# Graph layers with residual norms, fp32: adjacency rows loaded ahead of x and summed later, transposes queued on their own, another order for the first two aggregations and for the last softmax

## The chip, the cores and the metric

The kernel runs on one core of one Trainium2 chip. The metric is the device time of one execution in microseconds (us), the median of several. The groups of runs were made on different chips, and their medians of the kernel before differ by up to 0.3% (1958.9 us in one, 1961.8 to 1964.8 us in the others), so kernels of different groups are compared by their ratio to the kernel before in the same rounds.

Engines are named as in the profile: PE (TensorE, matmuls), PEld (its weight loads), DVE (VectorE), ACT (ScalarE), POOL (GpSimd), SP (it issues the DMA transfers). A line of a timeline has start and duration in us, engine, line of kernel.py, operation, tiles written<-read, shapes, and xN where N instructions are merged. L90 is the helper that issues the work of ACT, DVE and POOL, L173 is the matmul (L177 where an experiment's kernel has four lines more above it).

Tiles: y and v are sums of products of layer 0 and layer 1; own is the output of layer 0 while it is built up, z the half of layer 0's aggregation that is kept apart from own; fifth is the copy of one of the seven products, to be added elsewhere; xT is x transposed, x1T the transposed output of layer 0; xT_s, xT_i, x1T_s, x1T_i, sa and tv are the sums and differences that the seven products need of xT, x1T, adj and y.

## The reference

64 graphs of 256 nodes with 512 features. Two layers, each with a residual and a layer norm:

```python
# layer 0
deg = sum(adj, -1);  agg = (adj @ x) / max(deg, 1e-6)
x = layernorm(x + relu(concat([x, agg]) @ W.T))
# layer 1
q, k = split(x @ Wqk);  v = x @ Wv
agg = adj @ (k * mask)
w = inv_scale * mask * sum(q * agg, -1)
x = layernorm(x + softmax(w, over the nodes)[:, None] * v)
```

## The kernel before

It takes the graphs in 32 pairs. Layer 0 of pair j is interleaved with layer 1 of pair j-1. Products of 2x2 blocks are done with seven multiplications in place of eight (two levels deep for some), so between the matmuls there are many small sums: on ACT (copies from a PSUM bank to SBUF or to another bank), on DVE (additions), on POOL (sums of inputs). A unit of the lists below ("i", "k", "s") is one or two calls of `mm`, and each call shows as two matmul instructions in the trace.

The matmuls stand in a fixed order. The work of the norms, softmaxes and row sums is put between them by a small scheduler that runs while the program is built: chains of steps with a rank; after each unit, `tick` issues the first step whose engine, by a simple cost model, will be free in time. On the chip every engine then takes its instructions in that order.

```python
    act = InOrder(tc, nc.scalar, clock,
                  lambda name, n: 0.07 + n / 1200 if name == "copy" else 0.2 + n / 1000)
    ...
    def tick():
        while not quiet[0]:
            for c in list(chains):
                if c[2][0] <= clock[0] and c[3][0][0].free <= clock[0] + room[c[3][0][0]]:
                    step(c)
                    break
            else:
                return
```

The row sums of adj (the degrees) are made on ACT from a tile "turn", the transposes of the finished layer-0 output go into a tile of the same name and from there by 16 transfers into x1T:

```python
    def degrees(j):
        ...
        def degree(k, t):
            act.activation(r[:, k, t], r[:, k, t], AF.Copy, accum_out=deg[:, k, t:t + 1])
        ...
        queue(2, "degrees", ...four of them..., (vec, invert))

    def norm0(j):
        ...
            turns = [(vec, lambda k=k, t=t: turn(k, t)) for t in range(NT)] if j < NP - 1 else []
            queue(1, "norm", *work, *norm_of(own[:, k], total), *turns)
```

The loop over the pairs (j > 1):

```python
            run("i k", i=i, k=k)
            send_scores(j - 2)
            run("i l k", i=i, k=k, l=open1)
            flush("norm")                       # what is left of the norm, transposes last
            fetch_scores(j - 2)
            places[0](range(16))                # turn -> x1T
            run("i k i k", i=i, k=k)
        ...
            load_x(j)
            load_rows(j + 1)
        ...
        run("m p p m p p m", m=m, p=p)          # p: first products with xT_s ("S2")
        ...
        queue(1, "sums", *sums_Y)               # sums of x1T
        T = sums_T(ys[j])                       # four differences tv (T1 to T4) from y
        degrees(j + 1)
        ...
        run("s s j s a b j c d j k e j", s=s, j=jj, k=k, **g)   # a to g: the aggregation
```

In the aggregation (`gather`), a and b end with additions to own on DVE; those of a read the bank that d writes again. d also needs T2, e needs T3, g needs T4.

## Time and profile before

| | kernel before |
|---|---|
| time | 1958.9 us median (1958.2 to 1963.1, 4 runs) |
| busy: PE, DVE, ACT, POOL | 96%, 79%, 67%, 46% |
| time lost between matmuls, all | 102.3 us |
| of it 0 to 45 / 45 to 63 / 63 to 105 us | 4.8 / 10.6 / 9.5 us |
| of it in the 28 pairs up to the last | 65.5 us |
| after the last matmul's end | 15.6 us |

"Lost" is the time between the starts of neighbouring matmuls less what it is undisturbed, as the prediction tells. The "28 pairs" are the same 28 x 216 matmuls in every kernel of this document, so the sums can be compared directly. (In the kernel before they run from 246 to 1903 us, a pair later than those of the prediction; hence 65.5 us here and 66.5 there.)

The prediction shows the shares, waits and timelines of this kernel.

### The profile page before, as it was taken

To read this page: it belongs to the slowest core of one execution; us is meant where nothing else is said; L and a number is where in the kernel's file an instruction comes from. 1 tells how busy PE (TensorE), PEld (TensorE's weight loads), DVE (VectorE), ACT (ScalarE), POOL (GpSimd) and SP (SyncE) were. 2 spreads that over 40 slices of the span, in tenths; PEclk is the share of its full clock that TensorE was granted. 3 is DMA by queue.
4 is the path that set the end of the run, shared out by engine and by line. 5 is a ranking of instruction groups with operands and counts; after the bars stand their busy time and mean duration, and the time that the engine had idled before them with its cause. 6 is when DMAs were issued, how large, how long until landed. Compare 5 with 4: busy or idle time off the path is not lost.

```text
span 1958.7 us, 24833 instructions
## 1 busy us (share of the span) xinstructions
PE 1882.4 (96%) x6980; PEld 1310.1 (67%) x6980; DVE 1556.1 (79%) x3185; ACT 1304.8 (67%) x3267; POOL 896.1 (46%) x1187
## 2 busy tenths in 40 slices
PE   9899999999999999999999999999999999999995
PEld 4567666667666676666676666666666666666674
DVE  7678877878787788878788878788878787878786
ACT  3467766676766676666776676777676766666775
POOL 4354534544435554435544445444345444355531
PEclk9899999999999999999999999999999999999998
DMA  6132343423343323333323333323434323434211
GB/s 216 37 75 94 88 112 81 113 74 96 91 114 82 101 81 100 92 92 103 83 94 99 98 93 102 79 94 87 113 82 113 78 93 90 113 81 113 72 53 49
DMA packets 389160, 182.30 MB, mean 93 GB/s; under 512 B 272160, under 2 KB 353696, under 8 KB 389024
## 3 DMA queue, kind: packets, MB, share of 16 engines
q1 hardware_dynamic: 389024, 180.72, 34.4%
q8 instruction: 57, 0.93, 0.2%
q14 instruction: 79, 0.65, 0.1%
HBM read 114.10 MB, written 34.06 MB: 76 GB/s over the span
## 4 chain that ended last, share of the span: by engine, by line
PE 64%; SPq 11%; DMA 9%; ACT 7%; DVE 7%; issue 2%; POOL 0%; ACTq 0%; DVEq 0%
PE bank L173 64%; SPq L178 11%; DMA turn<-adj 6%; DMA x1T<-turn 3%; ACT junk L90 2%; ACT turn L90 2%; ACT bank L90 2%; DVE own L90 1%; DVE v L90 1%; DVE tv L90 1%; DVE y L90 1%; ACT own L90 1%; DVE turn L90 1%; ACT rstd L90 1%; DMA xT<-x_t 1%
## 5 line engine op out<-in xcount | busy, mean ns | idle before, releaser
L90 ACT COPY bank<-bank 128x256 f32<-128x256 f32 (+1 forms) x768 | 336.1, 438 | 218.1 <-PE bank L173 211.2
L90 DVE TENSOR_TENSOR y<-bank,y 128x512 f32<-128x512 f32 x256 | 170.5, 686 | 144.2 <-ACT y L90 138.6
L90 ACT ACTIVATE junk<-own,less 128x512 bf16<-128x512 f32 x252 | 181.7, 721 | 62.4 <-DVE less L90 59.4
L173 PE MATMUL bank<-tv,sa 128*128 128x256 f32 x768 | 199.4, 388 | 6.9 <-DVE own L90 3.1
L90 ACT ACTIVATE own<-own,shift,rstd 128x512 f32<-128x512 f32 x256 | 198.5, 812 | 3.4 <-DVE shift L90 3.4
L90 POOL TENSOR_TENSOR x1T_s<-x1T,x1T_s 128x512 f32<-128x512 f32 x32 | 48.5, 1517 | 316.5 <-PE bank L173 316.5
L173 PEld LDWEIGHTS bank<-tv,sa 128*128 128x128 f32 x768 | 142.0, 191 | 69.9 <-issue 22.4
L90 ACT COPY y<-bank 128x512 f32<-128x512 f32 x192 | 109.3, 587 | 98.8 <-PE bank L173 92.9
L173 PE MATMUL bank<-w,x1T_s 128*128 128x512 f32 (+1 forms) x384 | 168.3, 521 | 0.0
L90 POOL TENSOR_TENSOR sa<-adj 128x256 f32<-128x256 f32 x128 | 95.8, 749 | 151.7 <-DMA adj<-adj_t 151.7
L90 POOL TENSOR_TENSOR x1T_i<-x1T_s 128x128 f32<-128x128 f32 x128 | 77.9, 608 | 188.8 <-DVE x1T_s L90 186.3
L90 POOL TENSOR_TENSOR x1T_i<-x1T 128x256 f32<-128x256 f32 x64 | 59.8, 934 | 223.8 <-DMA x1T<-turn 203.3
L173 PE MATMUL bank<-t,xT_s 128*128 128x512 f32 (+1 forms) x384 | 158.5, 522 | 1.7 <-ACT own L90 1.7
L173 PE MATMUL bank<-t,x1T_s 128*128 128x512 f32 (+1 forms) x384 | 158.1, 521 | 0.3 <-ACT y L90 0.3
L173 PE MATMUL bank<-t_i,x1T_i 128*128 128x256 f32 x512 | 153.4, 382 | 4.3 <-ACT bank L90 3.8
L90 DVE TENSOR_TENSOR v<-bank,v 128x512 f32<-128x512 f32 x186 | 119.1, 681 | 48.0 <-PE bank L173 48.0
L173 PE MATMUL bank<-t_i,xT_i 128*128 128x256 f32 x512 | 153.1, 381 | 3.9 <-ACT bank L90 3.8
L173 PE MATMUL bank<-w,xT_s 128*128 128x512 f32 (+1 forms) x384 | 153.6, 522 | 0.0
L173 PEld LDWEIGHTS bank<-t_i,x1T_i 128*128 128x128 f32 x512 | 95.6, 190 | 76.3 <-issue 67.6
L173 PEld LDWEIGHTS bank<-t_i,xT_i 128*128 128x128 f32 x512 | 95.3, 190 | 62.1 <-issue 50.9
L90 ACT COPY own<-bank 128x512 f32<-128x512 f32 x128 | 71.3, 582 | 95.4 <-PE bank L173 70.8
L173 PE MATMUL bank<-w,x1T_i 128*128 128x256 f32 x384 | 116.3, 385 | 17.7 <-ACT bank L90 14.7
(155 smaller groups left out, 4638.8 us busy)
## 6 DMA issues: line engine op xcount, KB each, us to landing
x<-x SPq DMA_DIRECT2D x64, 512.0 KB, 4.7
xT<-x_t SPq DMA_DIRECT2D x62, 512.0 KB, 5.4
x1T<-turn SPq DMA_DIRECT2D x496, 64.0 KB, 2.3
out<-own SPq DMA_DIRECT2D x62, 512.0 KB, 3.2
adj<-adj_t SPq DMA_DIRECT2D x64, 256.0 KB, 3.8
turn<-adj SPq DMA_DIRECT2D x64, 256.0 KB, 4.9
row<-d SPq DMA_DIRECT2D x31, 256.0 KB, 4.7
wqk<-wqk_t SPq DMA_DIRECT2D x4, 512.0 KB, 5.1
```

The lines of the kernel that those rows point to most:

```text
L90: return self.tc.keep_in_program_order(getattr(self.engine, name)(out, *args, **kwargs))
L173: tc.keep_in_program_order(nc.tensor.matmul(ps, a, b, start=start, stop=True, skip_group_check=True))
L178: return tc.keep_in_program_order(nc.sync.dma_start(out, in_))
```

## The change

Its intent: no engine in order should stand behind work that waits for something late. The core of the diff (the first two aggregations and the end are cut; signatures too):

```diff
-                  lambda name, n: 0.07 + n / 1200 if name == "copy" else 0.2 + n / 1000)
+                  lambda name, n: 0.07 + n / 1200 if name == "copy" else (0.3 if n == F else 0.2) + n / 1000)
...
-            turns = [(vec, lambda k=k, t=t: turn(k, t)) for t in range(NT)] if j < NP - 1 else []
-            queue(1, "norm", *work, *norm_of(own[:, k], total), *turns)
+            steps = work + norm_of(own[:, k], total)
+            if j < NP - 1:
+                def last(k=k, scale=steps[-1][1]):
+                    scale()
+                    queue(1.5, "norm", *[(vec, lambda k=k, t=t: turn(k, t)) for t in range(NT)], ready=act.free + 0.4)
+                steps[-1] = (act, last)
+            queue(1, "norm", *steps)
...
-            load_x(j)
             if j + 1 < NP:
                 load_rows(j + 1)
+            load_x(j)
...
-        if j != 1 and j < NP - 1:
-            degrees(j + 1)
+        if j == 0:
+            degrees(1)
...
-            run("s s s a b c d e g f", s=s, **g)                 # pair 0
+            early.append(inner("P1", Xs[1], W0, pw[0], u, lambda fifth: early[1](fifth)))
+            run("s s a b s d c e i g f", s=s, i=early[0], **g)
...
-                run("s s j s a b j c d j k e j", s=s, j=jj, k=k, **g)
+                run("s s j s a b j", s=s, j=jj, k=k, **g)
+                if j < NP - 1:
+                    degrees(j + 1)
+                run("c d j k e j", s=s, j=jj, k=k, **g)
...
-    run("l", l=open1)                                            # end
     send_scores(j - 1)
+    run("l", l=open1)
```

In the first two pairs three of the four differences tv are also made after the first aggregation steps in place of before them, other work is kept out there (`quiet`), and the preparation of w0 is split. At the end the last softmax but one is queued earlier, and two reciprocals go before the last additions to v.

## The prediction

> **What bounds the kernel now.** I began with the page's shares and slices, for the kernel as a whole.
>
> ```profile
> span 1958.7 us, 24833 instructions
> ...
> PE 1882.4 (96%) x6980; PEld 1310.1 (67%) x6980; DVE 1556.1 (79%) x3185; ACT 1304.8 (67%) x3267; POOL 896.1 (46%) x1187
> ...
> PEclk9899999999999999999999999999999999999998
> ```
>
> TensorE (PE) is the bound, at full clock except near the start and the end. The change removes no product, so all it can win is time in which PE stands still. Busy time understates that, because the ends of matmuls are modelled, so I took start times from the timeline: undisturbed, a 256-column matmul starts 0.216 us after the one before and a 512-column one 0.429 us (each product is two such instructions). Whatever two starts are further apart is lost. Over all 6980 it sums to 102.3 us: about 27 before 190 us, 66.5 from 190 to 1850 us (28 pairs of batches, 59.4 us each, 2.38 a pair), some 7 to 1945 us, and then the tail without PE. 1958.7 - 102.3 = 1856 us is the floor for this set of products with the present head and tail.
>
> Next, who waits for whom:
>
> ```profile
> ACT turn L90 <- DMA turn<-adj: 50.1, 30, 3.7
> ...
> PE bank L173 <- ACT bank L90: 41.5, 60, 3.8
> ```
>
> PE waits mostly for ScalarE (ACT) copies out of a bank; ACT itself is only 67% busy, but 30 times, once a pair, it waits for the rows of adj (tile "turn"). A typical pair, a lucky pair, and the last pair, which makes no row sums, in stretches:
>
> ```profile
> 309.30:368.70 59.40, 57.60 (x217) 40.31 (x216) 47.53 (x98) 40.54 (x102) 27.13 (x37) 1.00 0.35 94
> 665.90:725.30 59.40, 58.76 (x223) 41.61 (x222) 47.67 (x99) 40.89 (x104) 29.64 (x40) 1.00 0.35 94
> 1853.20:1903.00 49.80, 49.80 (x187) 35.00 (x186) 40.50 (x83) 34.20 (x83) 19.64 (x26) 1.00 0.26 65
> ```
>
> First figure after the comma is PE's busy time. In the last pair PE never stops (0.04 us lost by start times). So the row sums are the suspect, and ACT's timeline in the typical pair shows them:
>
> ```profile
> 329.03 0.59 ACT L90 COPY own<-bank 128x512 f32<-128x512 f32 x1 [2.15 <-PE bank L173]
> 331.83 0.42 ACT L90 ACTIVATE turn<-turn 128x256 f32<-128x256 f32 x1 [2.21 <-DMA turn<-adj]
> ...
> 333.05 0.36 ACT L90 COPY bank<-bank 128x256 f32<-128x256 f32 x1
> ...
> 336.35 0.37 ACT L90 COPY bank<-bank 128x256 f32<-128x256 f32 x1
> ```
>
> ACT is held 2.21 us by the first row sum; the two bank copies behind it come late, and PE loses 0.41 us at 333.55 and 1.08 us at 336.86, then 0.27 us at 338.83 for a z copy. Per pair by start times: about 0.3 + 0.8 + 0.27 there.
>
> The other regular loss is 0.90 us in every pair, just after a pair's start:
>
> ```profile
> 310.05 0.36 ACT L90 COPY bank<-bank 128x256 f32<-128x256 f32 x1 [0.94 <-PE bank L173]
> 310.32 1.52 ACT L90 ACTIVATE own<-own,shift,rstd 128x512 f32<-128x512 f32 x2
> 311.74 0.58 ACT L90 COPY bank<-bank 128x512 f32<-128x512 f32 x1
> ```
>
> Two scalings of the previous norm stand in front of a copy that PE waits for until 312.38. Their shift was ready on VectorE (DVE) only at 307.69, behind two transposes of 0.7 us.
>
> The start has large single waits, of which the first aggregation is the worst:
>
> ```profile
> 49.36 1.13 PE L173 MATMUL bank<-tv,sa 128*128 128x256 f32 x4 [1.42 <-DVE tv L90]
> 52.73 1.79 PE L173 MATMUL bank<-tv,sa 128*128 128x256 f32 x4 [2.24 <-DVE own L90]
> 55.19 2.08 PE L173 MATMUL bank<-tv,sa 128*128 128x256 f32 x4 [0.68 <-ACT z L90]
> 57.94 1.22 PE L173 MATMUL bank<-tv,adj 128*128 128x256 f32 x2 [0.68 <-ACT z L90]
> ```
>
> 10.6 us are lost between 45 and 63 us, 9.5 between 63 and 105.
>
> **What the Trainium skill says.** "TensorE: Matmul & The Clock Gate", section "Architectural detail: the array is 16× 32×32, not 1× 128×128", has ScalarE and VectorE as strict FIFOs; the trace agrees, since the copy at 333.05 follows the held row sums although its bank was written by about 331. The same page, "Part 1: The HAM clock gate", has PE's clock halved after a few us of idleness: from 53 to 63 us matmuls start every 0.425 us instead of 0.216, so the waits at 49 to 53 us cost twice. "ScalarE: Activation LUTs", section "What ACT_TABLE_LOAD costs", gives 186 ns + 0.833 ns an element and 93 ns for each per-partition operand: 706 ns for the squares and 799 ns for the scalings of 512. The trace has 721 and 812; the schedule's own cost was 0.2 + 0.512 = 0.712, and the change's 0.3 + 0.512 = 0.812 fits the scalings. "Trainium Kernel Development and Optimization", section "Key Constraints", has all queues share the same 16 DMA engines: the rows were issued at 325.93, behind x (1 MB, issued 324.32 and 324.98, landed 328.37 and 331.11), and landed at 331.81.
>
> **The change part by part.**
>
> *Rows before x, row sums later.* The rows (0.5 MB) need about what x's first half took, 4.0 us: landing about 329.5 to 330 instead of 331.8 to 332.5. The sums are queued only after the aggregation's first two steps, at about 334.5 to 339 in this pair's time; the squares of the finished pair take the early ACT slots. I wrote ACT's order down with the durations of the trace (copies 0.27 and 0.51 us apart, squares 0.85, row sums 0.40): the second copy ends near 334.9, PE wants it at 335.3; the z copy ends near 336.1, PE wants it at 337.0. So the 0.3, 0.8 and 0.27 go, nearly. I leave 0.2 a pair, for VectorE's additions to own, which have no slack there (0.14 to 0.36 us in some pairs). About 1.35 + small ones, less 0.2: 1.25 a pair, times 30 = 37 us. x lands later by some 2 us but is needed some 20 us on.
>
> *Transposes as own chains.* At the end of a pair the second norm's shift now passes the first norm's two transposes (rank 1 against 1.5), so with 1.4 us of assumed delay its scalings fit one product step earlier: after the copy at 308.76 instead of after that at 310.05. By the same durations: scalings start 309.0 and 309.7, the copy of the other unit is pushed to 310.45 to 310.8, and PE, which wants its bank at 310.7, loses about 0.15 plus the 0.1 that each restart costs, in place of 0.90. 0.64 times 30 = 19 us. The higher ACT cost moves some other steps by one slot; I found none that then blocks.
>
> *The first two aggregations.* Pair 0: no w1 or row-sum work among the last products (VectorE spent 43.0 to 45.1 on w1), three of the four differences after the first steps, a product between each two steps on one bank. Following VectorE (0.7 to 1.6 us a step while GpSimd is busy), the wait before the second u step shrinks to about 1.8 us, the others to near 0, and the end of the aggregation comes near 54 us instead of 61.5, with one product step of pair 1 already made: 8 us, half of it the slowed clock. Pair 1: one of two z waits and the own wait go, 1.6 us; its norm, flushed at about 76 us, follows sooner by some 2 us, but the 3.9 us wait there stays in large part. The late T3 and S3 in pair 0 free VectorE before 28.8: the 1.85 us wait at 29.89 goes. Sum 13 us.
>
> *The tail.* Scores sent before the last products: VectorE is 0.9 us earlier at the differences for which PE waits 1.08 us at 1910.57: 0.8. The earlier last softmax hardly moves its divide, since VectorE has no gap from 1926 to 1937. The two reciprocals go before the four v additions (1939.2 to 1941.5), so that the shift at 1943.20 comes about 1.1 us sooner. Sum 2 us.
>
> Total 37 + 19 + 13 + 2 = 71 us: 1958.4 - 71 = 1887 us. Some of it will come back as waits that I don't see; I say 1890.
>
> **The rivals.**
>
> *Another wait takes over in each pair.* PE ahead by 1 to 2 us meets x1T sooner: its last transfer lands at 325.84, GpSimd's first sum of it ends at 326.90, PE wants it at 329.7; slack of 2.8 us less 0.9. VectorE is at 79% and has no slack at own. Against it: the last pair and the lucky pair (1.3 us lost, of which 0.90 and 0.27 are the two other waits) run the same work without such a wait. If half of the gain comes back, 1920.
>
> *The scalings still block.* If the shift misses its slot, or the bank copy behind the scalings stops PE as long as now, the 19 us stay: about 1908.
>
> *Only the order of the transfers counts.* If rows land in time anyway, making them later wins nothing, or the four sums (1.6 us) now hold the copies of the next steps. For it: lucky pairs lose nothing at the copies. Against: ACT has 2.2 us of idle time to refill. Costs up to 0.5 a pair, 15 us: 1905.
>
> *The start gains little,* if the clock is halved all the same by a 2 us wait: 6 us less, 1896.
>
> **Range and chances.** The centre is 1890. Losing one of the large terms gives 1905 to 1912; with all waits in the pairs gone it is near 1876. Range 1874 to 1914. 2% faster is 1919, which needs 39 of 71 us: both terms in the pairs would have to fail by half. Faster 0.86, within 2% 0.13, slower 0.01.
>
> **What would show it.** Right: the ACT wait for the rows gone from the list of waits (50 us to under 5); PE's wait for ACT bank copies from 41 to under 15 us; a pair 57.4 us long instead of 59.4; scalings before the copy at a pair's start; PEclk at 9 or more in the slices from 40 to 100 us; the first aggregation ending before 56 us. Wrong: pairs of 58.5 us or more, with a wait for own, POOL or x1T where ACT's was; a wait of 0.9 us still at each pair's start.

## More of the kernel before

One line more is needed for comparison, the page's chain that ended last, followed back from the end, as shares of the span by engine. SPq and DMA are transfers and their issue:

```profile
PE 64%; SPq 11%; DMA 9%; ACT 7%; DVE 7%; issue 2%; POOL 0%; ACTq 0%; DVEq 0%
```

A fifth of the chain runs through transfers. By the page they are mostly the rows and x1T (6% and 3%; the 11% of their issue is not told apart): with ACT held by a row sum, the wait for a transfer becomes a wait of PE.

## The result, and the profile after

| | before | after |
|---|---|---|
| median | 1958.89 us (1958.17 to 1963.12, 4 runs) | 1902.51 us (1900.91 to 1903.15, 4 runs) |
| ratio | 1 | 0.9707 (95%: 0.969 to 0.9723) |
| lost between matmuls, all | 102.3 us | 43.5 us |
| 0 to 45 / 45 to 63 / 63 to 105 us | 4.8 / 10.6 / 9.5 | 4.2 / 3.3 / 8.8 |
| 28 pairs | 65.5 us | 23.0 us |
| after the last matmul's end | 15.6 us | 17.0 us |

A ratio is the mean time of one kernel's fast runs over that of the other's of the same rounds, so it is not quite the ratio of the two medians.

The gain is 56 us where 68 were predicted; the time lies within the predicted range. The lines of the page of the kernel after that answer to those of before:

```profile
span 1901.3 us, 24809 instructions
...
PE 1867.6 (98%) x6980; PEld 1312.8 (69%) x6980; DVE 1548.6 (81%) x3185; ACT 1297.9 (68%) x3267; POOL 898.5 (47%) x1187
...
PEclk9999999999999999999999999999999999999998
...
PE 73%; DVE 16%; ACT 5%; issue 2%; DMA 2%; POOL 2%; SPq 0%; ACTq 0%; DVEq 0%; POOLq 0%
```

PE has the same 6980 matmuls. The clock is at 9 tenths or more in every slice but the last. In the chain, transfers fell from 20% to 2% and DVE rose from 7% to 16%: what PE waits for has changed hands.

From the list of waits after (who waits for whom: us in all, how often, the longest):

```profile
PE bank L173 <- ACT bank L90: 4.7, 3, 3.9
...
PE bank L173 <- DVE own L90: 3.2, 13, 0.3
```

ACT's wait for the rows (50.1 us before) is no longer in the list at all, PE's wait for ACT's bank copies fell from 41.5 us to 4.7 (3.9 of it one wait at the start), and additions to own have grown among PE's waits: before there were four (3.1 us, the longest of 2.2 us at the start), now there are 13 short ones. The list leaves out shorter waits still; by start times those for own sum to 9.3 us in the 28 pairs, where it was 1.9 before.

ACT's timeline in a typical pair (start, duration, instruction; in brackets the idle time before it):

```profile
315.69 0.36 ACT L90 COPY bank<-bank 128x256 f32<-128x256 f32 x1 [0.42 <-PE bank L173]
...
318.42 0.72 ACT L90 ACTIVATE junk<-own,less 128x512 bf16<-128x512 f32 x1
...
319.14 0.36 ACT L90 COPY bank<-bank 128x256 f32<-128x256 f32 x1
319.44 0.41 ACT L90 ACTIVATE turn<-turn 128x256 f32<-128x256 f32 x1
...
320.94 0.59 ACT L90 COPY z<-bank 128x512 f32<-128x512 f32 x1 [1.00 <-PE bank L173]
```

The row sum at 319.44 comes behind the two bank copies and waits for nothing. ACT is now early: before the z copy it waits 1.00 us for PE.

PE waits elsewhere in this pair, first in the aggregation. DVE's and PE's timelines there:

```profile
318.25 0.69 DVE L90 TENSOR_TENSOR tv<-y,tv 128x512 f32<-128x512 f32 x1
318.85 1.65 DVE L90 SCALAR_TENSOR_TENSOR own<-bank,rdeg,own 128x256 f32<-128x256 f32 x4
```

```profile
319.77 1.13 PE L173 MATMUL bank<-tv,sa 128*128 128x256 f32 x4 [0.24 <-DVE own L90]
```

DVE runs without a gap from 309.9 to 323 us. The additions to own start when the last difference tv is done, and PE's next product on that bank starts 0.40 us late (0.24 in the profile's own count, which takes idle time only).

And at a pair's start, ACT, DVE and PE in turn:

```profile
294.19 1.52 ACT L90 ACTIVATE own<-own,shift,rstd 128x512 f32<-128x512 f32 x2
295.61 0.85 ACT L90 COPY bank<-bank 128x256 f32<-128x256 f32 x2
```

```profile
297.54 1.30 DVE L90 STREAM_TRANSPOSE turn<-own 128x512 f32<-128x512 f32 x2
298.76 1.39 DVE L90 TENSOR_TENSOR bank<-bank,fifth 128x256 f32<-128x256 f32 x4
```

```profile
299.93 1.96 PE L173 MATMUL bank<-t,xT_s 128*128 128x512 f32 x4
```

The scalings now stand before the copy at 295.61, as predicted, and PE loses 0.32 us there in place of 0.90. But at 299.93 PE starts its first S2 product 0.28 us late. This wait is new (0.2 us in all 28 pairs before, 4.4 us after). The profile's record of the releaser there is GpSimd's xT_s. That sum did end at 299.87. But there is a second reading: the ACT copy of that bank to own ran from 299.20, when the first bank addition let it, and the additions stood behind two transposes on DVE. Which one holds was left to an experiment.

The first aggregation, PE's timeline:

```profile
48.56 2.94 PE L173 MATMUL bank<-tv,sa 128*128 128x256 f32 x12 [1.76 <-DVE tv L90]
51.33 0.59 PE L173 MATMUL bank<-t_i,xT_i 128*128 128x256 f32 x2
```

One wait is left of the four before, and the next pair's products are already in between.

### The profile page after: what moved, and what is told of

It reads as the page before. It is cut to its first block, busy times and chain, and to the rows that moved or that the text cites.

```text
span 1901.3 us, 24809 instructions
## 1 busy us (share of the span) xinstructions
PE 1867.6 (98%) x6980; PEld 1312.8 (69%) x6980; DVE 1548.6 (81%) x3185; ACT 1297.9 (68%) x3267; POOL 898.5 (47%) x1187
## 4 chain that ended last, share of the span: by engine, by line
PE 73%; DVE 16%; ACT 5%; issue 2%; DMA 2%; POOL 2%; SPq 0%; ACTq 0%; DVEq 0%; POOLq 0%
PE bank L173 73%; DVE own L90 7%; DVE tv L90 4%; DVE y L90 3%; ACT own L90 2%; DMA adj<-adj_t 2%; POOL sa L90 1%; ACT junk L90 1%; DVE less L90 1%; ACT y L90 1%; POOL xT_s L90 1%; DVE z L90 0%; SPq L178 0%; ACT agg L90 0%; ACT rstd L90 0%
## 5 line engine op out<-in xcount | busy, mean ns | idle before, releaser
L90 POOL TENSOR_TENSOR x1T_s<-x1T,x1T_s 128x512 f32<-128x512 f32 x32 | 53.3, 1665 | 277.3 <-PE bank L173 277.3
L90 POOL TENSOR_TENSOR x1T_i<-x1T 128x256 f32<-128x256 f32 x64 | 55.6, 870 | 234.3 <-DMA x1T<-turn 221.6
L173 PE MATMUL bank<-t,x1T 128*128 128x512 f32 x256 | 130.4, 592 | 0.0
```

Source lines behind the costliest of these rows:

```text
L90: return self.tc.keep_in_program_order(getattr(self.engine, name)(out, *args, **kwargs))
L173: tc.keep_in_program_order(nc.tensor.matmul(ps, a, b, start=start, stop=True, skip_group_check=True))
```

## The experiments

Theory: ACT and DVE work in order. Before, ACT stood behind row sums that waited for a transfer, and behind two scalings that came late; the change removes both. Then PE, sooner by 1.5 us a pair, meets DVE, and part of the gain comes back as waits for own and S2. Rivals: only the order of the transfers counts (or only the place of the sums); the waits that are left are independent of each other and can be taken one by one.

All twelve runs gave correct results. Lost time in the 28 pairs by the product that starts late (from start times; "pair start": the product on the bank copied behind the scalings; "behind sums": the two products on x1T_i and w; "aggregation": tv,sa, which is the z copy and own; waits of under some 0.05 us and small others left out):

| kernel | median us | ratio to before (95%) | lost in 28 pairs | pair start | behind sums | aggregation | S2 |
|---|---|---|---|---|---|---|---|
| before | 1958.89 | 1 | 65.5 | 25.3 | 29.8 | 8.9 | 0.2 |
| after | 1902.51 | 0.9707 (0.9690 to 0.9723) | 23.0 | 8.9 | 0 | 9.3 | 4.4 |
| a_same (after again) | 1900.75 | 0.9691 (0.9669 to 0.9712) | 24.0 | 9.0 | 0 | 9.6 | 5.3 |
| u_order | 1901.86 | 0.9679 (0.9663 to 0.9695) | 22.2 | 8.9 | 0 | 8.9 | 4.1 |
| u_later | 1901.64 | 0.9677 (0.9659 to 0.9694) | 25.8 | 8.9 | 2.0 | 10.3 | 4.0 |
| u_both | 1941.71 | 0.9880 (0.9864 to 0.9897) | 60.4 | 8.9 | 43.6 | 4.1 | 3.3 |
| u_turns | 1911.37 | 0.9723 (0.9709 to 0.9738) | 31.5 | 25.3 | 0 | 5.9 | 0 |
| u_ends | 1913.35 | 0.9752 (0.9737 to 0.9766) | 23.6 | 9.0 | 0.2 | 8.9 | 4.2 |
| u_cost | 1902.60 | 0.9697 (0.9680 to 0.9713) | 23.4 | 9.0 | 0 | 9.3 | 5.0 |
| i_tlate | 1902.20 | 0.9698 (0.9681 to 0.9716) | 23.5 | 9.0 | 0 | 10.1 | 4.3 |
| i_tl2 | 1901.86 | 0.9691 (0.9675 to 0.9707) | 23.4 | 8.9 | 4.9 | 0 | 9.6 |
| i_fifth | 1893.73 | 0.9654 (0.9635 to 0.9674) | 15.9 | 9.0 | 0 | 6.5 | 0.2 |
| i_pair1 | 1898.46 | 0.9680 (0.9662 to 0.9699) | 23.8 | 9.0 | 0 | 10.3 | 4.5 |
| i_all2 | 1887.11 | 0.9617 (0.9602 to 0.9631) | 12.8 | 5.7 | 5.9 | 0 | 0.2 |

The aggregation's 8.9 us before are 7.2 for the z copy, also behind the row sums, and under 2 for own; in all other lines they are for own or, in i_tlate, for T2. Each line is one trace, and the kernel after, traced twice, gives 23.0 and 24.0, so differences of 1 us say nothing.

All edits are to the kernel after.

**u_order: x ahead of the rows again.**

```diff
+            load_x(j)
             if j + 1 < NP:
                 load_rows(j + 1)
-            load_x(j)
```

> The kernel after with x loaded ahead of the rows again, row sums still queued late. My theory (ScalarE stands in order behind row sums that wait for a transfer): the rows land near 332 us in a pair's time and the sums are wanted only from 334.5, so no wait comes back: 1902 us, within 2 of the kernel after. Rival 'only the order of the transfers counts': about 1.2 us a pair come back, 1930 or more, with ScalarE waiting for the rows as before.

It is as fast as the kernel after, and no wait for the rows comes back. So the order of the transfers alone is not what counts, as long as the sums stand late.

**u_later: the row sums at their old place.**

```diff
-        if j == 0:
-            degrees(1)
+        if j != 1 and j < NP - 1:
+            degrees(j + 1)
...
-                run("s s j s a b j", s=s, j=jj, k=k, **g)
-                if j < NP - 1:
-                    degrees(j + 1)
-                run("c d j k e j", s=s, j=jj, k=k, **g)
+                run("s s j s a b j c d j k e j", s=s, j=jj, k=k, **g)
```

> The kernel after with the row sums queued at their old, earlier place, rows still loaded ahead of x. Theory: the rows land about when the first sum is wanted, ScalarE waits at most 0.5 us a pair for them, but the four sums (1.6 us) now stand ahead of the aggregation's bank copies: 0.1 to 0.4 us a pair, 1906 to 1914 us. Rival 'only the order counts': 1902. Rival 'only the place of the sums counts': 1930 or more.

I missed here: it too is as fast as the kernel after. ACT does wait for the rows, as its line in the list of waits shows,

```profile
ACT turn L90 <- DMA turn<-adj: 12.9, 19, 1.9
```

but 19 times in place of 30 and for a quarter of the time, and of that PE sees 2.0 us in all: the copies behind the sums had enough time to spare.

**u_both: both undone.**

> The kernel after with both undone, x first and the sums early. Theory: the waits of the kernel before behind the row sums come back at 1.1 to 1.25 us a pair, 30 pairs: 1935 to 1940 us, and ScalarE waits about 2 us a pair for the rows. Rival 'VectorE is the limiter now and hides part of it': below 1925.

```profile
ACT turn L90 <- DMA turn<-adj: 66.8, 29, 3.7
```

Now the loss is back, 36 us in the pairs (60.4 less 24.0), and the time is 2.0% above the kernel after (0.9880 over 0.9691). The term was right, with 39 us for 30 pairs where 37 were predicted. But its two halves are not two gains: either one is enough, and the second adds nothing that these runs resolve.

**u_turns: the transposes in the norm's chain again.**

```diff
+            turns = [(vec, lambda k=k, t=t: turn(k, t)) for t in range(NT)] if j < NP - 1 else []
+            queue(1, "norm", *work, *norm_of(own[:, k], total), *turns)
```

(in place of the lines of the diff above)

> The kernel after with the transposes back at the end of the norm's own chain. Theory: the scalings fall one product step later and the wait of 0.90 us at each pair's start comes back in place of 0.32: 0.58 x 30 = 17 us, 1920. The wait for the first S2 product (0.16 us a pair) may go with it, because PE then is later: 1915. Rival 'scalings are not what holds PE there': 1902.

ACT's and PE's timelines at the start of the same pair:

```profile
296.19 0.36 ACT L90 COPY bank<-bank 128x256 f32<-128x256 f32 x1 [0.94 <-PE bank L173]
296.45 1.52 ACT L90 ACTIVATE own<-own,shift,rstd 128x512 f32<-128x512 f32 x2
297.88 0.58 ACT L90 COPY bank<-bank 128x512 f32<-128x512 f32 x1
```

```profile
298.51 0.70 PE L173 MATMUL bank<-t_i,xT 128*128 128x256 f32 x2 [0.64 <-ACT bank L90]
```

The wait of 0.90 us is back in each pair, 25.3 us in 28 pairs as before: at its own place the part is worth 25.3 - 9.0 = 16.3 us, what was predicted. But the whole difference is 7.5 us: with PE held at the pair's start, the S2 wait vanishes (5.3 to 0), and that for own shrinks (9.6 to 5.9). So about half of what this part wins is missing again within the same pair (by the times a little less: against u_order and u_later of the same rounds the part is worth 9.6 us). The kernel before and u_both show the same without the late row sums: there, too, the transposes bring only 5.1 us (65.5 less 60.4; u_both's new start and end don't touch the pairs, as u_ends will show).

The two waits go by different paths, and the traces tell them apart. Up to the addition that PE waits for at own, DVE works off 17 instructions without a gap. In the kernel after, in u_turns and in i_fifth they begin 2.97 us after the same product in every pair, so this work moves along with PE. But it takes 9.39 to 9.92 us, and PE's delay follows that length (correlation 0.99 over the 28 pairs of each of these runs). What varies is how GpSimd's sums lie to it. The pair shown, DVE and GpSimd in the kernel after:

```profile
312.44 1.17 DVE L90 TENSOR_TENSOR own<-own,fifth 128x512 f32<-128x512 f32 x1
```

```profile
312.34 0.72 POOL L90 TENSOR_TENSOR x1T_i<-x1T 128x256 f32<-128x256 f32 x1 [7.72 <-DMA x1T<-turn]
```

The addition ends at 313.61, 0.55 us after GpSimd's sum; where no sum is running it takes 0.69 us. In 21 of its 32 places in the kernel after a sum was running as it began, and in all 21 it ended 0.55 us after that sum's end. The mean length of the 17 instructions is 9.71 us in a_same and 9.59 in u_turns; times 28 that is 3.4 of the 3.7 us by which own differs. So what is missing at own comes from when DVE's work and GpSimd's sums meet, and not from a PE that comes too soon for a fixed plan of DVE.

**u_ends: the start and the end as in the kernel before** (the order of the first two aggregations, late differences, `quiet`, w0, last softmax; the diff is that of the change, reversed).

> The kernel after with its start (order of the first two aggregations, late differences, quiet, w0 in two parts) and its end (last softmax, scores, last additions) as in the kernel before; the pairs between as in the kernel after. Theory: 7.7 us come back between 45 and 63 us with a clock below 0.7 there, 1.85 us at 29.9, 1 at the second pair, 2 at the end: 12 to 13 us, 1913 to 1915 where the kernel after takes 1901. Rival 'the start gained from the transposes and rows, not from its own order': below 1907.

Between 45 and 63 us 10.6 us are lost again, as before (3.3 after), and 3.1 us at the wait for the last total; in the traces all of it makes 8.7 us (10.1 more lost, 1.4 less after the last matmul), by the ratios 12. The rival falls. One thing stands against my sum: the wait of the second pair at 74 us is 2.45 us here and 4.09 in the kernel after. Something in the new start makes it longer; that PE simply comes to it sooner is likely, but not shown.

**u_cost: ACT's old cost.**

```diff
-                  lambda name, n: 0.07 + n / 1200 if name == "copy" else (0.3 if n == F else 0.2) + n / 1000)
+                  lambda name, n: 0.07 + n / 1200 if name == "copy" else 0.2 + n / 1000)
```

> The kernel after with ScalarE's old cost (0.2 us plus 1 ns an element for a 512 activation, the trace has 0.1 more). Theory: the cost only shifts some steps by one slot; within 3 us of the kernel after, 1901. Rival 'the scalings go one slot sooner only because of it': the 0.9 us wait at each pair's start comes back in part, 1906 or more.

No difference, at any of the places. The scalings' slot comes from the chains, not from the cost.

**a_same: the kernel after, again.**

> The kernel after, unchanged, so that the partial kernels have a figure for it from their own chip and rounds. 0.968 to 0.972 of the kernel before.

0.9691, as expected.

**i_tlate: late differences in every pair.**

```diff
-        T = sums_T(ys[j], T_late if j < 2 else None)
+        T = sums_T(ys[j], T_late)
```

> The kernel after with the late differences (T2, T3, T4 after the first steps on the banks) in every pair's first aggregation, not only in the first two pairs. Theory (VectorE, full from 313.5 to 323 us in the pair shown, is what PE now waits for): the additions to own come 1.9 us sooner, the wait for own of 0.31 us a pair goes, 8 to 9 us less: 1893 to 1895 where the kernel after takes 1902.5. Rival 'the wait moves on to the next product of the aggregation (its T2)': within 2 us of the kernel after.

The rival was right. DVE and PE in this run:

```profile
315.83 0.68 DVE L90 TENSOR_TENSOR x1T_s<-x1T 128x512 f32<-128x512 f32 x1
316.55 0.69 DVE L90 TENSOR_TENSOR x1T_s<-x1T_s,x1T 128x512 f32<-128x512 f32 x1
317.16 0.87 DVE L90 SCALAR_TENSOR_TENSOR own<-bank,rdeg,own 128x256 f32<-128x256 f32 x2
317.94 0.69 DVE L90 TENSOR_TENSOR tv<-y,tv 128x512 f32<-128x512 f32 x1
```

```profile
318.69 1.13 PE L173 MATMUL bank<-tv,sa 128*128 128x256 f32 x4 [0.19 <-DVE tv L90]
```

The scheduler filled the place that I made with two sums of x1T, so PE waits as long as before, for T2 now. That is a fault of the experiment as much as of the theory, hence i_tl2 below.

**i_fifth: two additions to v after the next pair's bank additions.**

```diff
-                vec.tensor_add(v[:, HF:], v[:, HF:], fifth)
+                late_fifth.append(lambda v=v: vec.tensor_add(v[:, HF:], v[:, HF:], fifth))
...
             run("i k i k", i=i, k=k)
+            add_late()
```

> The kernel after with the two additions v<-v,fifth of each pair made after the bank additions of the next pair instead of before its last two transposes. Theory: transposes and bank additions come 0.8 us sooner on VectorE, the wait for the first S2 product (0.16 us a pair) goes: 4 us less. Rival 'that wait is for GpSimd's xT_s, as the profile's label has it': no change, because xT_s isn't touched.

```profile
294.57 1.29 DVE L90 TENSOR_TENSOR v<-bank,v 128x512 f32<-128x512 f32 x2 [1.61 <-PE bank L177]
295.77 1.29 DVE L90 STREAM_TRANSPOSE turn<-own 128x512 f32<-128x512 f32 x2
297.98 1.63 DVE L90 TENSOR_TENSOR bank<-bank,fifth 128x256 f32<-128x256 f32 x4 [0.91 <-PE bank L177]
```

The transposes come directly behind the two additions that free a bank, and DVE now waits 0.91 us for PE before the bank additions. The S2 wait is gone (5.3 to 0.2), with xT_s untouched: GpSimd's sum ends at 299.65 in this run, and PE starts S2 at 299.43, before that. So the label was wrong, and the order of DVE's work was the cause. The loss in the pairs fell by 8 us, twice what I expected, because the wait for own fell as well (9.6 to 6.5). The path is that of u_turns: the 17 instructions of DVE before own are 9.61 us long in the mean here, as against 9.71, which times 28 is 2.9 of the 3.1 us; their meeting with GpSimd's sums has shifted (of DVE's instructions `less<-sum`, which end 0.02 us after a sum of GpSimd when they meet one, 81 of 126 are held up here and 93 in a_same).

**i_pair1: in the second pair, the forced end of the norm and of the masks later.**

```diff
             run("m p p m p p m", m=m, p=p)
-            flush("norm")
-            places[0](range(16))
...
         run("q q q", q=q)
+        if j == 1:
+            flush("norm")
+            places[0](range(16))
+            load_rows(2)
+            load_x(1)
         flush("w0")
         run("r q r m", m=m, q=q, r=r)
+        if j == 1:
+            flush("mask")
+            sumsM[0] = adj_sums(0)
```

> The kernel after with, in the second pair alone, the forced end of the first norm and of the masks moved from before the S3 products to after them. Theory: the 4.09 us wait at 74.30 us is ScalarE working off a square, four scalings and three masks (6 us) in one piece; spread over the products it falls to 1 to 2 us, 2 to 4 us less in all. Rival 'ScalarE has that work all the same': the wait stands 3 us later.

The wait fell from 4.09 to 2.00 us, and 5.4 us in place of 8.1 are lost between 63 and 105 us. What the long wait costs besides itself can be read from PE's windows of the kernel after (from:to, length, busy time, granted clock, share of DMA, GB/s):

```profile
48.50:51.00 2.50, 2.44 (x11) 1.00 0.00 0
68.00:74.00 6.00, 2.37 (x8) 0.87 0.05 9
74.00:78.00 4.00, 3.70 (x9) 0.50 0.61 97
```

After the wait of 1.92 us at 48.56 the clock is full. After that of 4.09 us at 74.30 it is half, for some 4 to 5 us. In this experiment, after 2.00 us, it stays full. Two waits close together can do it as well: in the kernel before, after 1.58 and 2.40 us with four matmuls between, matmuls started at half the pace from 53.9 us.

**i_tl2: late T3 and T4, and the sums of x1T queued only behind the steps on the banks.**

```diff
-        if j > 1:
-            queue(1, "sums", *sums_Y)
...
-        T = sums_T(ys[j], T_late if j < 2 else None)
+        T = sums_T(ys[j], T_late)
+        if j > 1:
+            T_late.pop(0)()
+            T_late.insert(0, lambda: None)
...
                 run("s s j s a b j", s=s, j=jj, k=k, **g)
+                queue(1, "sums", *sums_Y)
```

> The kernel after with only the repair of the first aggregation that the late differences alone did not make: T3 and T4 after the steps on the banks, and the sums of x1T queued only after these steps. The earlier run left the wait in place because two x1T sums took the freed place on VectorE and PE then waited for T2. Theory: with that place kept, the wait for own (9.2 us over the pairs in the trace of the kernel after that was run again) goes and nothing follows it at once: 8 us less, 1893. Rival 'VectorE has the work all the same, so the next product that needs it waits (S2, 5.5 us now)': the S2 wait grows by half of what is won, 1897 or more.

The wait for own is gone entirely (9.6 to 0), and the kernel is not faster: S2 takes 9.6 us in place of 5.3, and 4.9 us appear at the first product on x1T_i. 23.4 us are lost in the pairs as against 24.0. The rival was right, more so than I had put it: not half of the gain goes, but all of it. The edit only moves DVE's work to a later place in the same pair, and PE meets it there. That is not so of every repair: i_fifth took away one wait and won more than it.

**i_all2: four repairs together** (late fifths, i_pair1, i_tl2, and no norm step between the two bank copies at a pair's start):

```diff
-            run("i l k", i=i, k=k, l=open1)
+            run("i", i=i)
+            quiet[0] = True
+            run("l", l=open1)
+            quiet[0] = False
+            run("k", k=k)
```

> The kernel after with four repairs: the fifth additions to v late (7 us less in its own run); the second pair's norm and masks spread (2.3 us less); in every pair's first aggregation T3 and T4 after the steps on the banks, and the sums of x1T queued only after these steps, so that they can't fill the place that is made (the wait for own, 0.24 us a pair once the fifths are late, goes: 6 us); and no norm step between the two bank copies at a pair's start, so that one scaling stands before the second copy and one behind it (the wait of 0.33 us a pair goes: 9 us). Theory: each wait stands by itself and PE has no other work to wait for: 1901 - 24 = 1877 us. Rival 'PE, sooner, meets the next wait (x1T sums, z copies)': 1885 or more.

It beats both kernels: 1887.1 us, 0.9617 of the kernel before and 0.8% under the kernel after (0.9617 over 0.9691). It is 10 us short of my sum, again in the rival's sense: own is at 0 and S2 at 0.2, but the wait at the pair's start is 5.7 us and not 0, and 5.9 us have come to the first product on x1T_i, where ACT now has three scalings in one piece (2.23 us from 281.77) ahead of a bank copy. The chain that ended last is now nearly PE alone:

```profile
PE 95%; DVE 3%; ACT 1%; issue 0%; DMA 0%; ACTq 0%; DVEq 0%
```

## Why the prediction was right or wrong

It was right in the outcome and in the two mechanisms, and 12.5 us too low, mostly because one term of the sum was taken at its own place only. A pair is 57.7 us long, between the 57.4 that it named as a sign of being right and the 58.5 of being wrong; its other signs came. Two small things in its working: the "about 27" us lost before 190 us should read 29, on which nothing rests, and its 706 and 799 ns are estimates from the page's formula, beside which it has the measured 721 and 812.

**Rows and row sums: 37 us predicted, 39 shown.** Undone together they cost 36 us in 28 pairs. The steps of the working came as told: second copy and z copy in time, ACT's wait for the rows gone. Two corrections. The change does the thing twice (u_order, u_later: either half is enough), where I had treated the rival "only the order" as losing up to 15 us. And the 0.2 us a pair that I left for own is 0.33 (9.3 us over 28), 4 us more. Own has in fact taken over the first of the three waits, the "0.3" before x1T_i (7.3 us in the 28 pairs): from the same product of layer 0 to the product on own's bank 12.78 us pass before and 12.73 after. With the transposes as before, the rows and sums are worth 34.0 us (65.5 less u_turns' 31.5).

**Transposes: 19 us predicted, 16 at its place, 8 in effect.** This is the step that failed: "0.64 times 30 = 19 us", in full. The wait at the pair's start fell from 0.90 to 0.32 us, where I had said about 0.25. But PE then runs into DVE: the S2 wait (0.16 to 0.19 us a pair) is new. And that for own is larger than it would be without (u_turns against a_same), because DVE's instructions before it are held up longer by sums of GpSimd. It is the first rival of the prediction, which I had noted with GpSimd, x1T and own as the places, and priced only at 3 us. For S2 I had looked at ACT alone and not written DVE's order down; i_fifth shows that DVE's order was the cause. The meeting of DVE and GpSimd I had not thought of at all.

**Start: 13 us predicted, 8.5 by the traces.** The first aggregation came as worked out: the one wait of 1.92 us (said: 1.8), products of pair 1 from 54.4 us (said: 54), no halved clock, and 7.3 us less lost between 45 and 63 us. The 1.85 us at 29.89 went too. In the second pair I had counted 3.6 us and 0.6 came: the z wait and the own wait went (1.5 us), but the wait at 74 us stayed, 3.94 to 4.09. With the old start and all else new it is 2.45 us (u_ends), so it is something in the new start that keeps it long. Another 1.3 us are a longer wait for the first weights at the head, which no part of the change touches.

**End: 2 us predicted, about 2 shown.** The wait for the last total fell from 3.1 to 0.3 us and that at the differences from 1.1 to 0.3; 1.4 us came back after the last matmul.

Together: 39 + 8 + 8.5 + 2 = 57.5 us against 56.4 measured; of the 71 predicted, 11 are missing in the transposes and 4.5 at the start.

What stays open: why i_tlate and i_tl2, which change the pairs, end at the same 23.4 to 23.5 us as the kernels that don't, and which part of the new start lengthens the wait at 74 us. That DVE's meeting with GpSimd sets the wait for own is read from the traces; no run here changed GpSimd's work alone.

## What to carry to other kernels

Work that waits for a transfer must not stand on an in-order engine ahead of copies that the bottleneck needs; loading it sooner or queueing it later are two ways of doing one thing, so count the gain once. A gain worked out at one wait is not yet the gain of the kernel: here half of one was given back (u_turns), another wholly (i_tl2), and a third doubled (i_fifth). Write down, for every other engine, when its next result is wanted if the bottleneck comes sooner, because waits in one loop hand their time on to each other; and look whether the same instruction always takes the same time, because its neighbours on another engine can lengthen it. Where the name of a releaser doesn't fit the times, follow the timeline of each engine, and test it by moving work that the name doesn't mention.

## What the Trainium skill lacked or had wrong

- "TensorE: Matmul & The Clock Gate", Part 1, gives the halved clock after an idle window of about 3.4 us; after single waits the runs agree (full clock after 1.92, 2.00 and, in u_ends at 80.57 us, 2.45 us; half after 4.09 us). But the kernel before and u_ends have half the clock after waits of 1.58 and 2.40 us with four matmuls between, neither of which is that long. It does not give what a wait costs besides its length: in the kernel after, the second 256-column matmul behind a wait of over 0.2 us started late as well, by 0.075 us in the median of 66.
- "VectorE: DVE Perf Modes", section "The three transpose paths", has one figure for the block transpose on VectorE, 311 ns for 128x128 bf16. For 128x512 in fp32 this kernel shows 0.66 to 0.71 us (124 in the kernel after, median 0.67; median 0.70 in the kernel before).
- No page that I read says how far a profile's name for a releaser can be trusted when several semaphores are waited for: at the first S2 product it named GpSimd's xT_s, and moving two VectorE additions alone took the loss there from 5.3 to 0.2 us.
